# The start of a four-layer image kernel: first gram by transposes, rows copied inside its chain, weights made later, two banks for the first mixing products

## The chip, the cores and the metric

The kernel runs on one core of a Trainium2 chip. The core has five instruction streams: TensorE (PE, with weight loads listed as PEld), VectorE (DVE), ScalarE (ACT), GpSimd (POOL) and SyncE (SP). SP issues nearly all of the transfers; POOL and ACT issue some. The metric is the device time of one execution in microseconds, the median of several runs. The profile shows one further execution, instruction by instruction; its span reaches from the first to the last instruction.

## The reference, cut to what matters

The input is `x`, 16 images of 64 channels of 128 x 128 pixels, in fp32. Four layers follow one another, each adding its result to its input after a group norm over pairs of channels:

```python
x = x + _L0_conv_ref(_gn(x), L0_conv_conv_w)       # gram = x x^T / N; y = gram x; out = conv_w y
x = x + _L1_conv_ref(_gn(x))                       # |Sobel x| + |Sobel y|, per channel
x = x + _L2_conv_ref(_gn(x), L2_conv_W, L2_conv_b) # 3x3 convolution of a shifted x
x = x + _L3_conv_ref(_gn(x), L3_conv_w_bin, ...)   # 3x3, 1x1, batch norm over all images, clip to 0..255
```

Layer 0 is linear once the 64 x 64 gram matrix of an image is known: the kernel turns it into one 64 x 64 mixing matrix, and the statistics of both first norms follow from the same gram. Layer 3's batch norm needs every image's product before any output can be written.

## The kernel before

**Staging.** Every image passes three stages, each over eight row chunks (`NS = 8` chunks of `R = 8` rows of each half of the image, the upper and lower half on 64 partitions each): `Front` (layer 0's mixing product and layer 1's Sobel), `Layer2` and `Layer3`. The loop `for step in range(steps)` at L911 walks through steps of four quarters `q`; image `b` enters `Front` at step `15 + 8 b`, with three steps of preparation before it, `Layer2` at 25 and `Layer3` at 35 (`starts`, L861). Nearly all instructions of these stages go through the class `InOrder` (its helper is L73, the line that the profile shows for them), which keeps each engine's instructions in the order of the program text. So the order of work on each engine is written out by hand, and nothing overtakes.

**The gram.** `Gram` (L407) runs ahead of `Front`. It loads image `b` with pixel rows on the partitions (`xr`: eight transfers of 512 KB, each of 8 channels, 512 bytes a run), and ACT copies each into `xw`, in which the channels of a pixel column lie side by side. Once all eight are copied, 128 small products accumulate the gram with the channel sums in `pg`, half of them into partitions 0 to 63 and half into 64 to 127. `gram_chain` (L301) then computes the mixing matrix `abd` and the coefficients `co` of the norm: a chain of small steps between PE and DVE through the tile `bank`, with two square roots on ACT inside `rstd`. Each `yield` lets the loop issue other work; `tick` (L252) moves the chain on once in a quarter. For images 0 and 1 the chain takes fewer yields than for later ones. Images 1 to 6 are loaded at two chunks a step (`pace`, L871), image 0 at one.

**Front.** `mix` (L470) makes a mixing product `po` of four rows per half (512 columns; `small_product`, L177, issues the two 64-channel halves, and each fp32 product appears in the trace as two instructions). The pool of `po` has one buffer, a PSUM bank. `prepare` (L475) lets ACT normalize a `po` into the ring `xh`, with the rows next to it copied to the neighbouring chunks. `sobel` (L527) is eight DVE instructions and two of ACT for each chunk; the first, `u<-xh`, needs the halo row of the next chunk's first `po`. At its first step, `Front` also loads two edge rows (`xe`) and stores one row of zeros, from `w0`, to a scratch tensor; this store waits for POOL's memset of `w0` (L216), and what follows it on SP waits behind it.

**Setup before the loop.** The constants `kc` (identity and averaging matrices, 611.5 KB) and five small vectors are loaded by SP (L119 to L133), the weights by ACT's queue. The weights of layer 3 are nine products of 64 x 64 through `bank` (L226) with six DVE copies into `w3` (L229); a sum of taps, two copies to `wm` and eight copies to the `packed` tiles complete the other weights (L214 to L238). POOL clears `xh`, `w2`, `w3`, `w0` and four difference tiles.

**The end.** After the last image's statistics, the kernel reads its two intermediate tensors from HBM, normalizes, adds and writes `out`.

Of the kernel before, what the change touches and what calls it, by code (L numbers as in the profile page):

```python
# [10 lines left out]
F32 = mybir.dt.float32  # L11
# [5 lines left out]
P = 128  # L17
# [3 lines left out]
R = 8  # L21
NS = HH // R
EARLY = 3
CP = 4
# [84 lines left out]
def tile_kernel(ctx: ExitStack, tc: tile.TileContext, x, cw_h, w2_t, b2, wbin_t, w1_t, b1, gamma, beta, consts, out):  # L109
# [6 lines left out]
    small = ctx.enter_context(tc.tile_pool(name="small", bufs=4))  # L116

    kc = cpool.tile([P, K_END], F32, name="kc")
    nc.sync.dma_start(kc, consts)  # L119

    def k(name):
        return kc[:, AT[name][0]:AT[name][1]]

    def load_const(src, shape, name):
        t = cpool.tile(shape, F32, name=name)
        nc.sync.dma_start(t, src)
        return t

    cwh = load_const(cw_h, [P, C], "cwh")
    b2_sb = load_const(b2, [P, 1], "b2_sb")  # L130
    b1_sb = load_const(b1, [P, 1], "b1_sb")
    gamma_sb = load_const(gamma, [P, 1], "gamma_sb")
    beta_sb = load_const(beta, [P, 1], "beta_sb")  # L133
    bn_sum = cpool.tile([P, B * NS], F32, name="bn_sum")
    bn_sq = cpool.tile([P, B * NS], F32, name="bn_sq")

# [35 lines left out]
    def cols(o):  # L172
        return slice(o * C, (o + 1) * C)
# [19 lines left out]


    xw = wpool.tile([P, W // 2, C + 1, 2], F32, name="xw")
    nc.gpsimd.memset(xw[:, :, C, :], 1.0)

    xh = wpool.tile([P, 3, R + 2, W + 2], F32, name="xh")
    nc.gpsimd.memset(xh, 0.0)
    junk = wpool.tile([P, R * W], mybir.dt.bfloat16, name="junk")  # L200
    wbd = wpool.tile([P, P], F32, name="wbd")
    nc.gpsimd.memset(wbd, 0.0)

    w2 = wpool.tile([P, 3, 3, P], F32, name="w2")
    w3 = wpool.tile([P, 3, 3, P], F32, name="w3")
    nc.gpsimd.memset(w2, 0.0)
    nc.gpsimd.memset(w3, 0.0)
    for slot, i, o, ky in TO_SLOTS:
        nc.scalar.dma_start(w2[i * C:(i + 1) * C, slot, :, o * C:(o + 1) * C], w2_t[:, ky])

    wm = wpool.tile([P, 3, P], F32, name="wm")
    for n in range(2):
        o = 1 - single(TO_SLOTS, n)[0]
        nc.vector.tensor_copy(wm[:, :, cols(o)], w2[:, n, :, cols(o)])  # L214
    w0 = wpool.tile([P, P], F32, name="w0")
    nc.gpsimd.memset(w0, 0.0)  # L216

    wb = work.tile([P, R + 1, W + 2], F32, tag="u", name="wb")
    wb = flat(wb)[0:C, 0:9 * C].rearrange("p (y x c) -> p y x c", y=3, x=3)
    w1 = work.tile([P, R, W + 2], F32, tag="e", name="w1", bufs=1)[0:C, 0, 0:C]  # L220
    nc.scalar.dma_start(wb, wbin_t)
    nc.scalar.dma_start(w1, w1_t)
    for ky in range(3):
        pw = sm(3 * C, rows=C).rearrange("p (k c) -> p k c", k=3)
        for kx in range(3):
            nc.tensor.matmul(pw[:, kx, :], wb[:, ky, kx, :], w1, start=True, stop=True)  # L226
        for slot, i, o, kk in TO_PAIRS:
            if kk == ky:
                nc.vector.tensor_copy(w3[i * C:(i + 1) * C, slot, :, o * C:(o + 1) * C], pw)  # L229

    packed = {}
    for name, w, table in (("pk2", w2, TO_SLOTS), ("pk3", w3, TO_PAIRS)):
        nc.vector.tensor_add(w[:, 2], w[:, 0], w[:, 1])
        packed[name] = wpool.tile([P, 2, C], F32, name=name)
        for n in range(2):
            o, i = single(table, n)
            for kx, half in ((1, i), (0, 1 - i)):
                nc.vector.tensor_copy(  # L238
                    packed[name][half * C:(half + 1) * C, n], w[i * C:(i + 1) * C, n, kx, o * C:(o + 1) * C]
                )  # L240

    diffs, twins = {}, {}
    for name in ("d2", "d3"):
        diffs[name] = wpool.tile([P, 2, CP, W + 2], F32, name=name)
        nc.gpsimd.memset(diffs[name], 0.0)
        twins[name] = wpool.tile([P, 2, CP, W + 2], F32, name=f"q{name}")
        nc.gpsimd.memset(twins[name], 0.0)


    chains = []  # L250
# [50 lines left out]
    def gram_chain(b, pg):  # L301
# [77 lines left out]
            yield  # L379
        pk = sm(1)  # L380
        small_product(pk, pp.rearrange("p s c -> p (s c)"), k("q"))
        yield
        bias = sv("bias")
        dve.tensor_copy(bias, av[:, 2:3])
        st1 = sv("st1", 2)
# [18 lines left out]
        dve.tensor_copy(co[:, 3:4], mean)  # L404
        lead[b] = abd, co

    class Gram:  # L407
        first, last = 0, NS + 1

# [3 lines left out]
        def at(self, i, q):  # L413
            b = self.b
            CG = C // 8
            if i < NS:
                if q == 0 and i != 1:
                    for m in range(i + (1 if i == 2 else 2) if i else 0, min(i + 3, NS)):
                        t = xin.tile([P, CG, W], F32, tag="xr", name=f"xr_{b}_{m}", bufs=3)
                        sp.dma_start(t, x[b].rearrange("c h w -> h c w")[:, m * CG:(m + 1) * CG, :])  # L420
                        self.xr[m] = t

                if q == 3 and i > 0:
                    for m in (0, 1) if i == 1 else (i,):
                        act.copy(
                            xw[:, :, m * CG:(m + 1) * CG, :].rearrange("p w c t -> p c w t"),
                            self.xr.pop(m).rearrange("p c (w t) -> p c w t", t=2),
                        )
                return
            n = 4 * (i - NS) + q  # L430
            if n == 0:
                self.pg = ps_g.tile([P, CP, W], F32, tag="g", name=f"pg_{b}")[:, 0, 0:C + 1]

            for _ in range(22 if n < 4 else 20 if n < 6 else 0):
                w = self.w
                s = w % 2
                pe.matmul(
                    self.pg[s * C:(s + 1) * C, :], xw[:, w // 2, 0:C, s], xw[:, w // 2, :, s],
                    start=(w < 2), stop=(w >= W - 2),
                )  # L440
                last[0] = s
                self.w += 1
            if n == 6:
                chains.append(gram_chain(b, self.pg))
# [5 lines left out]
    class Front:  # L450
# [17 lines left out]
            self.xs[i] = t  # L468

        def mix(self, i, g):  # L470
            po = ps_po.tile([P, CP, W], F32, tag="po", name=f"po_{self.b}_{i}_{g}")
            small_product(po, self.abd, self.xs[i][:, g * CP:(g + 1) * CP, :])
            self.po[i, g] = po

# [389 lines left out]
    def run(stage, b, i, q):  # L864
        if 0 <= b < B and stage.first <= i <= stage.last:
            if (stage, b) not in live:
                live[stage, b] = stage(b)
            live[stage, b].at(i, q)


    pace = {}  # L871
    at = 0
    for b in range(B):
        half = 1 <= b <= 2 * EARLY
        pace[b] = at, 2 if half else 1

        at += (NS // 2 if half else NS) + {0: 4, 2 * EARLY: 2}.get(b, 0)
    last_one = NS * (B - 1) + starts[0][1]
    steps = last_one + NS + 1

# [27 lines left out]
            loaded.append((yt, rt))  # L908
            fetched[0] += 1

    for step in range(steps):  # L911
        for q in range(4):
            for b in range(B):

                i = step - starts[2][1] - NS * b
                if 0 <= i < NS and q in (0, 2):
                    live[Front, b].sobel(i, f"first of {q}")
                if q == 3:
                    run(Layer2, b, step - starts[1][1] - NS * b, "first of 3")
            for stage, at in starts:  # L920
                for b in range(B):
                    run(stage, b, step - at - NS * b, q)
            if q == 3:
                for b in range(B):
                    run(Layer2, b, step - starts[1][1] - NS * b, "last of 3")
            for b in range(B):
                at, n = pace[b]
                for m in range(n):
                    v = 4 * n * (step - at) + n * q + m
                    run(Gram, b, v // 4, v % 4)  # L930
# [100 lines left out]
```

## Time and profile before

| what | value |
|---|---|
| median of 3 runs | 2827.53 us (2825.04 to 2830.61) |
| the profiled execution | 2829.05 us |
| its span | 2827.3 us |
| PE, DVE, ACT, POOL busy | 2241.5, 2200.4, 2120.5, 884.3 us |
| first gram's products on PE | 27.39 to 37.73 us |
| first Sobel instruction of image 0 on DVE | starts at 59.68 us |
| last stretch, without PE | 2381 to 2827.3 us, 414 GB/s |

A row of the page's groups or of a timeline names the line, the engine, the operation, the tiles as out<-in, the shapes and a count; after it stand the busy time, and in square brackets the idle time of the engine before it with what ended this. `SPq` marks the issue of a transfer, not its duration. PEclk is the clock that was granted to TensorE, as a share of full speed.

### The profile page before, as it was taken

The page shows a single profiled execution, that of the slowest core. Times are in us where ns is not written, and L with a number is a line of the kernel's source. Part 1 is how long each engine was busy: PE and PEld are TensorE (multiplying, and loading weights), DVE is VectorE, ACT ScalarE, POOL GpSimd, SP SyncE. Part 2 cuts the span into 40 slices and gives each one's busy share as a digit, 9 for nine tenths or more (in the row PEclk, how much of TensorE's full clock was granted, in tenths as well). Part 3 has the DMA queues.
Part 4 walks back from the last instruction along what each step waited for, and adds up shares of the span by engine and source line. Part 5 has one row for each costly group of instructions (what it writes and reads, how often), then busy time and mean ns, then how long its engine had stood idle before and what let it go on. Part 6 is the DMA issues. An engine that isn't in the chain of part 4 may idle for free. (4 is left out here: it accounts for less than half of the span.)

```text
span 2827.3 us, 46297 instructions
## 1 busy us (share of the span) xinstructions
PE 2241.5 (79%) x14772; PEld 1157.1 (41%) x14772; DVE 2200.4 (78%) x3758; ACT 2120.5 (75%) x3171; POOL 884.3 (31%) x1326
## 2 busy tenths in 40 slices
PE   4568899999999999999999999999999995000000
PEld 2333444545453535363646363566666641000000
DVE  3999999898989898989898989999996434333332
ACT  4666779888888888888888888998997666333332
POOL 1035433343434343434343434454444300000000
PEclk8678999999999999999999999999999997555555
DMA  6788978888888888888888877888877668999999
GB/s 166 192 219 227 235 199 237 213 232 205 229 209 224 213 221 215 220 216 223 215 221 216 220 183 191 207 207 213 208 209 186 156 201 285 419 420 420 420 420 391
DMA packets 688880, 685.95 MB, mean 243 GB/s; under 512 B 61744, under 2 KB 590144, under 8 KB 688640
## 3 DMA queue, kind: packets, MB, share of 16 engines
q1 hardware_dynamic: 662656, 614.42, 73.7%
q0 software_dynamic: 24576, 68.12, 9.8%
q8 instruction: 119, 1.95, 0.3%
q14 instruction: 121, 0.99, 0.1%
q10 hardware_dynamic: 1408, 0.46, 0.1%
HBM read 346.23 MB, written 268.44 MB: 217 GB/s over the span
## 5 line engine op out<-in xcount | busy, mean ns | idle before, releaser
L73 PE MATMUL two<-d,w 128*64 128x508 f32 (+2 forms) x2560 | 894.2, 588 | 5.8 <-DVE d L73 5.8
L73 PE MATMUL two<-d,wi 128*64 128x508 f32 (+3 forms) x1536 | 620.1, 577 | 0.0
L73 POOL DMA_DIRECT2D qd<-d x512 | 269.8, 529 | 870.8 <-issue 318.4
L73 PE MATMUL two<-qd,pk 128*64 128x512 f32 (+1 forms) x1024 | 520.3, 589 | 3.2 <-DMA qd<-d 2.1
L73 POOL TENSOR_SCALAR edges<-v,co 64x8 f32<-64x8 f32 x512 | 348.8, 681 | 357.9 <-ACT v L73 248.7
L73 PEld LDWEIGHTS two<-d,w 128*64 128x64 f32 x2560 | 305.3, 136 | 285.5 <-issue 194.7
L73 PE MATMUL po<-x,abd 128*64 128x512 f32 x1024 | 369.8, 629 | 61.6 <-ACT xh L73 60.6
L73 DVE TENSOR_TENSOR d<-v 128x512 f32<-128x512 f32 (+1 forms) x512 | 345.9, 678 | 75.3 <-issue 36.0
L73 PE MATMUL one<-v,w 128*64 128x508 f32 (+2 forms) x1600 | 394.7, 578 | 0.0
L73 PE MATMUL one<-v,wi 128*64 128x508 f32 (+3 forms) x1536 | 391.4, 593 | 0.0
L73 ACT COPY qd<-d 64x512 f32<-64x512 f32 x512 | 315.3, 616 | 30.1 <-DVE d L73 23.7
L73 DVE SCALAR_TENSOR_TENSOR e<-e 128x1032 f32<-128x1032 f32 (+1 forms) x256 | 312.7, 1222 | 0.0
L73 ACT ACTIVATE xh<-po,co 128x128 f32<-128x128 f32 (+1 forms) x480 | 275.1, 621 | 40.8 <-PE po L73 38.8
L73 DVE SCALAR_TENSOR_TENSOR y<-two,c 128x1024 f32<-128x1024 f32 x128 | 155.8, 1217 | 132.0 <-ACT v L73 44.2
L73 PEld LDWEIGHTS two<-d,wi 128*64 128x64 f32 x1536 | 195.7, 136 | 145.2 <-issue 97.7
L73 POOL TENSOR_SCALAR v<-v,kc 128x9 f32<-128x9 f32 x256 | 249.7, 988 | 11.9
L73 PEld LDWEIGHTS one<-v,w 128*64 128x64 f32 x1600 | 171.9, 137 | 159.3 <-issue 97.5
L73 ACT ACTIVATE v<-x,co 128x512 f32<-128x512 f32 (+2 forms) x368 | 234.9, 704 | 0.0
L73 PEld LDWEIGHTS one<-v,wi 128*64 128x64 f32 x1536 | 163.0, 139 | 154.2 <-issue 110.1
L73 ACT ACTIVATE u<-u 128x1024 f32<-128x1024 f32 x128 | 135.5, 1058 | 96.7 <-DVE u L73 96.3
L73 DVE SCALAR_TENSOR_TENSOR u<-xh 128x1170 f32<-128x1170 f32 x128 | 175.5, 1371 | 12.2 <-ACT xh L73 9.8
L73 PEld LDWEIGHTS po<-x,abd 128*64 128x64 f32 x1024 | 110.8, 140 | 174.3 <-ACT xh L73 93.1
(154 smaller groups left out, 3476.0 us busy)
## 6 DMA issues: line engine op xcount, KB each, us to landing
xr<-in_x SPq DMA_DIRECT2D x128, 512.0 KB, 6.6
x<-in_x SPq DMA_DIRECT2D x256, 256.0 KB, 4.2
x_d<-u SPq DMA_DIRECT2D x512, 128.0 KB, 3.6
y_d<-y SPq DMA_DIRECT2D x512, 128.0 KB, 4.3
x_d<-x SPq DMA_DIRECT2D x496, 128.0 KB, 2.5
qd<-d POOLq DMA_DIRECT2D x256, 130.0 KB, 3.1
qd<-d POOLq DMA_DIRECT2D x256, 129.8 KB, 3.6
v<-x_d SPq DMA_DIRECT2D x448, 72.1 KB, 3.0
```

Source lines behind the costliest of these rows:

```text
L73: return self.tc.keep_in_program_order(call(*args, **kwargs))
```

## The change

`first_gram` replaces `Gram` for image 0. The image comes in the layout of `Front` (16 transfers of 256 KB with 4 KB runs). For each of eight chunks, PE turns eight 128 x 128 squares with the identity into two PSUM banks (`turned`), DVE and ACT each copy one half into `xw`, and the 16 products of a chunk follow those of the next chunk's transposes. A Sqrt on a dummy value comes first on ACT. Then the first step of `Front` 0 is issued, then the eight `xr` loads of image 1 (into buffers of the tag `x3`, whose earlier readers are the transposes), and the chain of image 0 runs in one go, with image 1's copies placed between its links on ACT, and two after it. The loop starts at step 13.

The identity columns of `kc` are loaded by SP; the rest of `kc` and all other constants and weights by POOL's queue, and the order of the memsets is changed: `w0` now follows the weights' loads. Layer 3's weight products and the other weights become two functions called in step 14 after quarter 1. `po_0_0` and `po_0_1` share one two-bank tile of the tag `two`. One yield of `gram_chain` is dropped for images 0 and 1.

```diff
-    nc.sync.dma_start(kc, consts)
...
+    sp.dma_start(kc[:, 0:P], consts[:, 0:P])
+    pool.dma_start(kc[:, P:K_END], consts[:, P:K_END])
+    for t, src in ((wb, wbin_t), (w1, w1_t), (cwh, cw_h)):
+        pool.dma_start(t, src)
...
+    pool.memset(wbd, 0.0)
...
+    pool.memset(w3, 0.0)
...
+    pool.memset(xh, 0.0)
+    pool.memset(w2, 0.0)
+    for t, src in ((b2_sb, b2), (b1_sb, b1), (gamma_sb, gamma), (beta_sb, beta)):
+        pool.dma_start(t, src)
+    for slot, i, o, ky in TO_SLOTS:
+        pool.dma_start(w2[i * C:(i + 1) * C, slot, :, o * C:(o + 1) * C], w2_t[:, ky])
+    w0 = wpool.tile([P, P], F32, name="w0")
+    pool.memset(w0, 0.0)
...
+    def weights_of_layer_3():
+        for ky in range(3):
+            pw = sm(3 * C, rows=C).rearrange("p (k c) -> p k c", k=3)
+            for kx in range(3):
+                pe.matmul(pw[:, kx, :], wb[:, ky, kx, :], w1, start=True, stop=True)
+            for slot, i, o, kk in TO_PAIRS:
+                if kk == ky:
+                    dve.tensor_copy(w3[i * C:(i + 1) * C, slot, :, o * C:(o + 1) * C], pw)
...
+    def other_weights():
+        for n in range(2):
+            o = 1 - single(TO_SLOTS, n)[0]
+            dve.tensor_copy(wm[:, :, cols(o)], w2[:, n, :, cols(o)])
...
         pk = sm(1)
         small_product(pk, pp.rearrange("p s c -> p (s c)"), k("q"))
-        yield
+        if b > 1:
+            yield
...
+    def first_gram():
+
+        pg = ps_g.tile([P, CP, W], F32, tag="g", name="pg_0")[:, 0, 0:C + 1]
+        src = []
+
+        t = sv("sd")
+        dve.memset(t, 1.0)
+        act.activation(t, t, AF.Sqrt)
+        for m in range(NS):
+            t = ring.tile([P, 2, CP, W], F32, tag="x3", name=f"x_first_{m}", bufs=NS + 2)
+            t = t.rearrange("p a j w -> p (a j w)")
+            for h in range(2):
+                sp.dma_start(t[h * C:(h + 1) * C], halves(x[0].rearrange("c h w -> (c h w)"), h, m * R, R))
+            src.append(t)
+        for m in range(NS + 1):
+            if m < NS:
+                two = ps_two.tile([P, 2, CP, W], F32, tag="two", name=f"turned_{m}").rearrange("p a j w -> p (a j) w")
+                for j in range(R):
+                    pe.transpose(two[:, j], src[m][:, j * P:(j + 1) * P], k("I"))
+                for h, copy in ((0, dve.tensor_copy), (1, act.copy)):
+                    copy(xw[:, m * R:(m + 1) * R, 0:C, h], two[:, :, h * C:(h + 1) * C])
+            if m > 0:
+                for w in range(2 * R * (m - 1), 2 * R * m):
+                    gram_product(pg, w)
+        run(Front, 0, Front.first, 0)
+
+        rows = []
+        for m in range(NS):
+            t = ring.tile([P, C // 8, W], F32, tag="x3", name=f"xr_1_{m}", bufs=NS + 2)
+            sp.dma_start(t, x[1].rearrange("c h w -> h c w")[:, m * C // 8:(m + 1) * C // 8, :])
+            rows.append(t)
+        for link, _ in enumerate(gram_chain(0, pg)):
+            if link in (2, 3, 4, 5, 6, 7):
+                rows_to_columns(1, link - 2, rows[link - 2])
+        for m in range(6, NS):
+            rows_to_columns(1, m, rows[m])
...
         def mix(self, i, g):
-            po = ps_po.tile([P, CP, W], F32, tag="po", name=f"po_{self.b}_{i}_{g}")
+            if self.b == i == 0:
+
+                if g == 0:
+                    self.two = ps_two.tile([P, 2, CP, W], F32, tag="two", name="po_0_0")
+                po = self.two[:, g]
+            else:
+                po = ps_po.tile([P, CP, W], F32, tag="po", name=f"po_{self.b}_{i}_{g}")
...
+    first_gram()
...
-    for step in range(steps):
+    for step in range(starts[2][1] - 2, steps):
...
+            if step == starts[2][1] - 1 and q == 1:
+                weights_of_layer_3()
+                other_weights()
```

More of the change, by code (lines that the diff above doesn't have):

```diff
@@ L118, in tile_kernel, with const @@
     kc = cpool.tile([P, K_END], F32, name="kc")
-    nc.sync.dma_start(kc, consts)
     def k(name):
         return kc[:, AT[name][0]:AT[name][1]]
[L124 to L133, printed above, removed]
+    def const(shape, name):
+        return cpool.tile(shape, F32, name=name)
+    cwh = const([P, C], "cwh")
+    b2_sb, b1_sb, gamma_sb, beta_sb = (const([P, 1], n) for n in ("b2_sb", "b1_sb", "gamma_sb", "beta_sb"))
     bn_sum = cpool.tile([P, B * NS], F32, name="bn_sum")
@@ L195, in tile_kernel @@
     xw = wpool.tile([P, W // 2, C + 1, 2], F32, name="xw")
[L196 to L216, printed above, removed]
+    pool.memset(xw[:, :, C, :], 1.0)
     wb = work.tile([P, R + 1, W + 2], F32, tag="u", name="wb")
@@ L220, in tile_kernel @@
     w1 = work.tile([P, R, W + 2], F32, tag="e", name="w1", bufs=1)[0:C, 0, 0:C]
[L221 to L240, printed above, removed]
+    sp.dma_start(kc[:, 0:P], consts[:, 0:P])
+    pool.dma_start(kc[:, P:K_END], consts[:, P:K_END])
+    for t, src in ((wb, wbin_t), (w1, w1_t), (cwh, cw_h)):
+        pool.dma_start(t, src)
+    junk = wpool.tile([P, R * W], mybir.dt.bfloat16, name="junk")
+    wbd = wpool.tile([P, P], F32, name="wbd")
+    pool.memset(wbd, 0.0)
+    w2 = wpool.tile([P, 3, 3, P], F32, name="w2")
+    w3 = wpool.tile([P, 3, 3, P], F32, name="w3")
+    pool.memset(w3, 0.0)
+    xh = wpool.tile([P, 3, R + 2, W + 2], F32, name="xh")
+    pool.memset(xh, 0.0)
[6 more added lines that the diff above has]
+    pool.memset(w0, 0.0)
     diffs, twins = {}, {}
@@ L244, in tile_kernel @@
         diffs[name] = wpool.tile([P, 2, CP, W + 2], F32, name=name)
-        nc.gpsimd.memset(diffs[name], 0.0)
+        pool.memset(diffs[name], 0.0)
         twins[name] = wpool.tile([P, 2, CP, W + 2], F32, name=f"q{name}")
-        nc.gpsimd.memset(twins[name], 0.0)
+        pool.memset(twins[name], 0.0)
+    def weights_of_layer_3():
[6 more added lines that the diff above has]
+                    dve.tensor_copy(w3[i * C:(i + 1) * C, slot, :, o * C:(o + 1) * C], pw)
+    wm = wpool.tile([P, 3, P], F32, name="wm")
+    packed = {}
+    def other_weights():
+        for n in range(2):
+            o = 1 - single(TO_SLOTS, n)[0]
+            dve.tensor_copy(wm[:, :, cols(o)], w2[:, n, :, cols(o)])
+        for name, w, table in (("pk2", w2, TO_SLOTS), ("pk3", w3, TO_PAIRS)):
+            dve.tensor_add(w[:, 2], w[:, 0], w[:, 1])
+            packed[name] = wpool.tile([P, 2, C], F32, name=name)
+            for n in range(2):
+                o, i = single(table, n)
+                for kx, half in ((1, i), (0, 1 - i)):
+                    dve.tensor_copy(
+                        packed[name][half * C:(half + 1) * C, n], w[i * C:(i + 1) * C, n, kx, o * C:(o + 1) * C]
+                    )
     chains = []
@@ L405, in gram_chain, with gram_product, rows_to_columns @@
         lead[b] = abd, co
+    def gram_product(pg, w):
+        s = w % 2
+        pe.matmul(
+            pg[s * C:(s + 1) * C, :], xw[:, w // 2, 0:C, s], xw[:, w // 2, :, s],
+            start=(w < 2), stop=(w >= W - 2),
+        )
+        last[0] = s
+    def rows_to_columns(b, m, t):
+        act.copy(
+            xw[:, :, m * C // 8:(m + 1) * C // 8, :].rearrange("p w c t -> p c w t"),
+            t.rearrange("p c (w t) -> p c w t", t=2),
+        )
+    def first_gram():
[31 more added lines that the diff above has]
+            rows_to_columns(1, m, rows[m])
     class Gram:
@@ L424, in at @@
                     for m in (0, 1) if i == 1 else (i,):
[L425 to L428, printed above, removed]
+                        rows_to_columns(b, m, self.xr.pop(m))
                 return
@@ L434, in at @@
             for _ in range(22 if n < 4 else 20 if n < 6 else 0):
[L435 to L441, printed above, removed]
+                gram_product(self.pg, self.w)
                 self.w += 1
@@ L868, in run @@
             live[stage, b].at(i, q)
+    first_gram()
     pace = {}
[L872 to L877, printed above, removed]
+    at = 12
+    for b in range(1, B):
+        pace[b] = at, 2 if b <= 2 * EARLY else 1
+        at += NS // pace[b][1] + (2 if b == 2 * EARLY else 0)
     last_one = NS * (B - 1) + starts[0][1]
@@ L925, in tile_kernel @@
                     run(Layer2, b, step - starts[1][1] - NS * b, "last of 3")
-            for b in range(B):
+            for b in range(1, B):
                 at, n = pace[b]
@@ L929, in tile_kernel @@
                     v = 4 * n * (step - at) + n * q + m
-                    run(Gram, b, v // 4, v % 4)
+                    if b > 1 or v >= 4 * NS:
+                        run(Gram, b, v // 4, v % 4)
+            if step == starts[2][1] - 1 and q == 1:
+                weights_of_layer_3()
+                other_weights()
             tick()
```

## The prediction

> **What bounds the kernel now.** I read the page first: the span, the busy digits by slice and the chain that ended last; then a table of busy times by stretch, then the timelines of the first 82 us, since every edit but one acts before step 16.
>
> ```profile
> span 2827.3 us, 46297 instructions
> PE   4568899999999999999999999999999995000000
> DVE  3999999898989898989898989999996434333332
> DMA 14%; ACT 1%; DVE 0%; PE 0%; issue 0%; SPq 0%; ACTq 0%
> ```
>
> The chain of the page starts at 2361 us and says only that the last 446 us are DMA. It does not reach the change. The stretches do (columns: length, busy time with count on PE, PEld, DVE, ACT, POOL; clock; DMA share; GB/s):
>
> ```profile
> 0.00:60.00 60.00, 23.27 (x330) 16.42 (x332) 13.92 (x64) 21.74 (x25) 9.79 (x15) 0.86 0.71 174
> 60.00:130.00 70.00, 42.23 (x610) 25.54 (x606) 64.99 (x102) 42.57 (x59) 0.40 (x2) 0.66 0.66 168
> 130.00:800.00 670.00, 617.33 (x4435) 285.56 (x4437) 621.65 (x1148) 554.67 (x843) 273.69 (x389) 0.95 0.86 222
> 800.00:2381.00 1581.00, 1558.67 (x9407) 829.54 (x9402) 1344.70 (x2319) 1345.10 (x2118) 600.39 (x921) 1.00 0.79 209
> 2381.00:2827.30 446.30, 0.00 (x0) 0.00 (x0) 155.15 (x129) 156.47 (x128) 0.00 (x0) 0.50 1.01 414
> ```
>
> DVE, then PE, is full from 60 to 2381 us; in the first 60 us no engine is. The instruction order of every engine after step 16 is the same in both kernels except around the second image's chain, so whatever the first Sobel step of image 0 gains or loses should arrive at the end whole. I call its start S (59.68 us now) and the start of the copy of the first gram E (37.79 us now). The timeline, in order of time:
>
> ```profile
> 6.46 14.68 SPq L73 DMA_DIRECT2D xr<-in_x  x8
> 22.55 0.48 SPq L73 DMA_DIRECT2D x_d<-w  x1
> 27.39 10.34 PE L73 MATMUL pg<-xw 128*64 128x65 f32 x256 [15.33 <-ACT xw L73]
> 37.79 0.23 DVE L73 COPY gs<-pg 128x65 f32<-128x65 f32 x1 [21.21 <-PE pg L73]
> 47.85 1.92 PE L73 MATMUL po<-x,abd 128*64 128x512 f32 x4
> 48.34 3.20 ACT L73 COPY xw<-xr 128x1024 f32<-128x1024 f32 x3
> 53.22 1.97 PE L73 MATMUL po<-x,abd 128*64 128x512 f32 x4 [3.44 <-ACT xh L73]
> 56.42 1.98 PE L73 MATMUL po<-x,abd 128*64 128x512 f32 x4 [1.23 <-ACT xh L73]
> 58.44 1.13 ACT L73 ACTIVATE xh<-po,co 128x512 f32<-128x512 f32 x2 [1.04 <-PE po L73]
> 59.68 1.38 DVE L73 SCALAR_TENSOR_TENSOR u<-xh 128x1170 f32<-128x1170 f32 x1 [9.85 <-ACT xh L73]
> ```
>
> So: 26 us of loads and copies with PE idle, 10.34 us of products in one piece, a chain of 10.44 us to its second Sqrt (48.23), three copies of image 1's rows in front of the first activation (3.20 us), and PE and ACT taking turns on one bank. From E to S it is 21.89 us.
>
> **What the Trainium skill says.** "TensorE: Matmul & The Clock Gate", Part 4, gives a transpose 390 ns alone and about 275 ns in a kernel, for bf16; the page's Terms say that the transpose mode is four times faster for FP32, and its section on LDWEIGHTS prices a load at columns / 1.2 GHz, so 107 ns for 128 columns. This trace holds no transpose. Part 1's two clock states are there: the same 65-column product pieces ran at 46 ns each (4.09 us for 88) and then 32 ns (5.40 us for 168). "DMA: Bandwidth & Descriptors", Specifications, wants 512 B runs for line rate; here 512 B rows of xr moved at 213 to 295 GB/s and the end's 4 KB rows at 414.
>
> **The change part by part.** All against the profiled execution: 2829.05 us around a span of 2827.3; the median of the runs, 2827.53, is 1.5 lower, and I take the difference over to it.
>
> *First gram.* Removed: eight xr loads, eight ACT copies, the wait until all have come. Added on SP: 64 KB of identity and 16 half loads of 256 KB in 4 KB rows; at 0.55 us an issue (1.10 for two) the first chunk is issued by 2.2 and its second half, begun at 1.67, lands 4.2 us later (median of the page's x row): 5.9. All 4.19 MB, with 0.75 MB of POOL's loads beside them, take 12 us at 414 GB/s, so the last chunk is there by about 15 to 16. On PE: 64 transposes T and 128 products, in the order T T G T G … G G. The products cost 10.34 us (1.29 a chunk). T is the unknown. Below: 0.107 us, the column load alone. Above: an ordinary fp32 product of 128 columns, two instructions of 0.25 us in the slow clock (four bank<-kc,vv took 1.01 us at 92.67), 0.50. I take 0.15, what one such instruction takes in the fast clock (0.60 us for four at 41.25), as the FP32 mode speaks for a single pass. The copies out of PSUM (DVE and ACT each 512 columns, near the 0.77 us of xh<-po) lie beside the next chunk's PE work; only the last shows. E = 5.9 + 64×0.15 + 10.34 + 0.77 = 26.6. PE is then the limit, not the loads.
>
> *Rows of image 1.* The eight copies (1.15 us each) leave the stretch after the chain: six stand on ACT between the two Sqrts (6.9 us in a gap of 8.2), two after. But their loads now queue on SP behind xe, behind the store of zeros from w0, and behind x_0, and the w0 memset has moved behind 14 DMA issues on POOL: 0.95 + 5.7 us of memsets + 14×0.52 (the qd<-d row) = 14 us; 20 if the six w2 issues with three runs a row cost three times that. Then 1.6 us of issues and 5.2 MB (x_0, xr, x_1) at 285 GB/s plus a latency: x_1 lands about 21 us after w0, at 35 to 41; row 5 at 30 to 36, before the second Sqrt at 37. The first activation moves to about 40, and five ACT pieces (0.45, 0.45, 0.76, 1.13, 1.13) are done by 44.
>
> *Two banks.* po_0_0, po_0_1 and po_1_0 no longer wait for ACT (3.44 and 1.23 us): by the rows above they end at E+11.98, +13.95 and +15.93.
>
> *Weights later.* This is not free. On PE nine products follow po_1_0 and stand before po_1_1; on DVE 16 instructions stand right before the first Sobel one. Three rounds of 0.90 (PE) and 0.72 (two DVE copies), with handovers, 5.1 us; then two wm copies 0.58, two adds 1.10, eight pk copies 1.58: 3.3. So S = E+15.93+8.4 = E+24.3. Before, they ran from 6.9 to 16.6 us under the loads at no cost; now they take back the two banks' gain and more (21.89 before).
>
> *Second chain.* One yield less: DVE waits once for pk's product, about 0.5 us; its tail moves before some Sobel work, same total.
>
> Sum: S = 26.6+24.3 = 50.9, 8.8 earlier, less 0.5: 8.3. Span 2819.0, profiled execution 2820.7, median 2819.2.
>
> **The rivals.** *All goes fast:* T 0.107 and products at 32 ns a piece (8.2 us): E = 21.8, S = 46.1, near the loads' own bound (x_1 at 35 + 1.98 + 8.4 = 45.4): 13 us less, 2814. For it: the loads do allow it. Against: the first pieces run at the slow clock.
>
> *Transposes about 0.21 to 0.28, or SP late:* load and stream one after the other at 1.2 GHz, 0.213, give E = 30.7 and a gain of 4; 0.275 gives none. A w0 at 24 us gives S = 24+31.3 = 55, again a gain of 4. Median 2823 to 2828.
>
> *Slower, by the price of a transpose:* place, PE between 6 us and E. From T = 0.28 nothing is left (E = 34.9), and from 0.37 it is slower by more than 0.2%. At 0.39 E is 42 and the median 2834; at 0.50, 2841. For it: no fp32 transpose is in the trace, the one number for bf16 alone is that large, and each loads new weights. Against: durations of overlapping instructions are longer than their spacing (LDWEIGHTS of two<-d,w: 136 ns mean, while the gram's pairs came every 40).
>
> **How the numbers follow.** Likeliest 0.42 (2815.5 to 2822), all fast 0.18, the middle case 0.25, slower 0.15. The runs before span 2825.04 to 2830.61, and 0.2% is 5.65 us, about what a measurement of this kernel can tell. Faster: the first two, and a little of the third less the likeliest's upper edge: 0.61. Same: 0.25. Slower: 0.14. The range goes from the fast case less 2 us of spread, 2812, to just short of the 0.39 case, 2832.
>
> **What would show it.** E near 26 and S near 51 in the new timeline; PE without long waits on DMA between 6 and E; 128-column transposes spaced 0.15 us, eight in 1.2; DVE's w3, wm and pk copies ending right at S, the first Sobel instruction released by DVE rather than by ACT; and the 2321 us from S to the last stretch (2381 − 60) unchanged. Wrong if transposes come in two instructions of 0.2 us, if PE's po waits for x_1 (then SP is the limit and the x_d<-w issue stands late), or if ACT's second Sqrt waits for a row.

## The result, and the profile after

| kernel | median (lowest to highest) | runs | ratio to before, 95% interval |
|---|---|---|---|
| after | 2825.27 us (2821.45 to 2827.68) | 20 | 0.9989 (0.9982 to 0.9996) |
| before, same chip | 2828.72 us (2821.70 to 2832.86) | 20 | |
| after, a second time | 2825.73 us (2824.57 to 2828.25) | 13 | 0.9993 (0.9985 to 1.0001) |
| before, same chip | 2828.02 us (2824.59 to 2833.95) | 25 | |

The change gives 3.4 us, and 2.3 us when measured again: within the 0.2% that the prediction called no difference to be told, though the first interval lies below 1. The forecast was 8.3 us. The profiled execution of after took 2827.62 us around a span of 2825.8; before's took 2829.05 around 2827.3.

The stretches of the start after the change, with the columns as in the table of before (length; busy time and count on PE, PEld, DVE, ACT, POOL; clock; DMA share; GB/s):

```profile
0.00:60.00 60.00, 34.66 (x398) 23.97 (x400) 17.68 (x71) 20.60 (x29) 17.98 (x29) 0.78 0.81 188
60.00:130.00 70.00, 39.25 (x592) 24.11 (x590) 64.21 (x101) 38.46 (x54) 0.40 (x2) 0.63 0.60 154
```

PE does 11.4 us more in the first 60 us (34.66 against 23.27). DVE has eight copies out of PSUM more, 0.69 us each (17.68 against 13.92 us in all), and is full no sooner. The timeline of after, in order of time, shows where the start stands:

```profile
1.18 15.28 SPq L73 DMA_DIRECT2D x_first<-in_x  x16
9.65 3.79 PE L73 MATMUL turned<-kc,x_first 128*128 128x128 f32 x16 [9.65 <-DMA x_first<-in_x]
14.52 1.09 PE L73 MATMUL turned<-kc,x_first 128*128 128x128 f32 x8
21.97 1.06 PE L73 MATMUL turned<-kc,x_first 128*128 128x128 f32 x8 [0.61 <-DMA x_first<-in_x]
42.40 0.20 ACT L73 ACTIVATE sd<-var 128x1 f32<-128x1 f32 x1 [0.56 <-DVE var L73]
45.58 1.15 ACT L73 COPY xw<-xr 128x1024 f32<-128x1024 f32 x1 [1.94 <-DMA xr<-in_x]
46.76 0.46 ACT L73 ACTIVATE xh<-pe,co 64x128 f32<-64x128 f32 x1
48.41 3.68 PE L73 MATMUL po<-x,abd 128*64 128x512 f32 x8 [4.46 <-ACT xh L73]
52.02 0.90 PE L73 MATMUL bank<-w,wb 64*64 64x64 f32 x6
59.43 0.79 DVE L73 COPY pk<-w 64x64 f32<-64x64 f32 x4
60.25 1.38 DVE L73 SCALAR_TENSOR_TENSOR u<-xh 128x1170 f32<-128x1170 f32 x1
```

The copy of the first gram starts at E = 31.24 us (37.79 before): 6.55 us gained. The first Sobel instruction starts at S = 60.25 us (59.68 before): all of it is given back, and 0.57 us more. A second profile of after has E = 31.23 and S = 58.80, two of before 59.68 and 59.35. Of the 1.45 us between the two profiles of after, 0.95 lie between the end of `po_1_0` and S: the same weight products took 0.90, 0.90 and 0.90 us in one and 0.63, 0.56 and 0.56 us in the other, where the granted clock from 52 to 56 us was 0.50 and 0.89. So the start is worth nothing within a microsecond, and the 2 to 3 us of the median come from elsewhere; the last experiments are about that.

Four readings follow from these lines. The first transposes wait 9.65 us for their chunk. Eight transposes take 1.09 us from the third chunk on, and 1.9 us in each of the first two. The write of `po_0_1`, which was to have its own bank, waits 4.46 us for ACT to read `po_0_0`. And the weights fill DVE up to S itself: the first Sobel instruction has no idle time before it.

### The profile page after: what moved, and what is told of

The parts are those of the page before. It is cut to its first block, busy times and chain, and to the rows that moved or that the text cites. A ratio compares the mean times of both kernels' runs of the same rounds, so it can differ in the third digit from the quotient of the medians.

```text
span 2825.8 us, 46448 instructions
## 1 busy us (share of the span) xinstructions
PE 2251.2 (80%) x14836; PEld 1162.2 (41%) x14836; DVE 2205.7 (78%) x3767; ACT 2115.0 (75%) x3171; POOL 893.3 (32%) x1340
## 3 DMA queue, kind: packets, MB, share of 16 engines
q8 instruction: 120, 1.97, 0.3%
```

## Experiments

"After" and "before" are whole kernels; an edit is against the one named. Ratios are to before on the same chip.

**The weights, both ways.** First, after with layer 3's three rounds (three products and two copies each) between the gram's chunks, and the other weights at the end of `first_gram`, ahead of the loop:

```diff
+    def weights_of_layer_3(taps_y):
+        for ky in taps_y:
...
+            if m in (3, 4, 5):
+                weights_of_layer_3([m - 3])
...
+        other_weights()
...
-            if step == starts[2][1] - 1 and q == 1:
-                weights_of_layer_3()
-                other_weights()
```

> The changed kernel with only the weights moved: layer 3's three rounds between the chunks of the first gram, the other weights on DVE between the end of the chain and the first Sobel step. Theory (the start counts whole, and DVE's weights hold the first Sobel step): S is then set by ACT's halo row of po_1_0, which ended at 53.3 us in the changed kernel's trace, so S near 53.5 to 54.5 instead of 60.25, and the median 6 to 7 us below the changed kernel's 2825.3, at 2818 to 2819.5. Rival (the difference between the kernels is made in the tail, where y waits for its store, and the start has slack): S moves the same, but the median stays at 2824 to 2827.

Measured: 2818.71 us (2814.82 to 2819.57), ratio 0.9966 (0.9952 to 0.9979). Its timeline:

```profile
19.07 0.56 PE L73 MATMUL bank<-w,wb 64*64 64x64 f32 x6
52.25 1.38 DVE L73 SCALAR_TENSOR_TENSOR u<-xh 128x1170 f32<-128x1170 f32 x1 [5.21 <-ACT xh L73]
```

A round between chunks costs PE 0.56 us. E is 31.41, as in after, though the three rounds took 1.7 us: PE waited only 0.40 us for later chunks in place of 1.52, and the first chunk happened to come 0.95 us earlier in this profile (8.70 against 9.65). S comes 8.0 us earlier (6.6 against the second profile of after) and waits for ACT, not for DVE's weights. It is 1.25 us before the expected 53.5, mostly since the last row's copy waited 0.71 us, not 1.94, for its load. The theory held: the median is 8.2 us below before on its own chip, which is 4.7 to 5.9 us more than after's two gains (6 to 7 expected).

Then the other way: in the kernel before, the setup's nine products and 18 DVE instructions for the weights go into step 14, with nothing else of the change:

```diff
-    for ky in range(3):
...
+            if step == starts[2][1] - 1 and q == 1:
+                weights_of_layer_3()
+                other_weights()
```

> The kernel before with one part of the change alone: the weights made in step 14, as in the changed kernel. Theory (on DVE they stand ahead of the first Sobel step and nothing hides them there): S goes from 59.68 to about 58.4 + 8.3 = 66.7, and the median rises by about 7 us, to 2835.5 (ratio 1.0025). Rival (slack later on takes it up): S rises but the median stays within 2 us of before.

Measured: 2833.4 us (2828.76 to 2835.39), ratio 1.0022 (1.0013 to 1.0031), S = 67.56. From its timeline:

```profile
66.73 0.79 DVE L73 COPY pk<-w 64x64 f32<-64x64 f32 x4
67.56 1.38 DVE L73 SCALAR_TENSOR_TENSOR u<-xh 128x1170 f32<-128x1170 f32 x1
```

It is 6.5 us slower, from a shift of S by 7.88, and the Sobel instruction again follows DVE's weights without idle time. This part of the change is a loss on its own, and of the size that the prediction gave it (8.4 us).

**Two tiles in place of one tile of two banks.** After, with `po_0_0` and `po_0_1` in two tiles of the tag `two`:

```diff
-                if g == 0:
-                    self.two = ps_two.tile([P, 2, CP, W], F32, tag="two", name="po_0_0")
-                po = self.two[:, g]
+                po = ps_two.tile([P, 2, CP, W], F32, tag="two", name=f"po_0_0_{g}")[:, 0]
```

> The changed kernel with po_0_0 and po_0_1 in two tiles of two banks each instead of two halves of one tile; all else as it is. Theory (the wait of 4.46 us in front of po_0_1 comes from the shared tile: a write to one half waits for ACT's read of the other): PE makes po_0_0, po_0_1 and po_1_0 in one piece, only x_1's landing between them, the weights start near 48 instead of 52.0, S near 56 instead of 60.25, median 3.5 to 4.5 us below the changed kernel. Rival (PE waited for something else that ended then, such as x_1 or the row copies): the wait stays and S stays at 60.

Measured: 2821.85 us (2819.29 to 2824.71), ratio 0.9983 (0.9975 to 0.9991). Its timeline:

```profile
42.24 3.05 PE L73 MATMUL po<-x,abd 128*64 128x512 f32 x8
46.82 1.08 PE L73 MATMUL po<-x,abd 128*64 128x512 f32 x4 [1.52 <-DMA x<-in_x]
47.45 2.79 ACT L73 ACTIVATE xh<-po,co 128x512 f32<-128x512 f32 x5
55.04 1.38 DVE L73 SCALAR_TENSOR_TENSOR u<-xh 128x1170 f32<-128x1170 f32 x1
```

Now both products of chunk 0 run in one piece, ahead of ACT, and what holds the third is a load. `po_1_0` ends at 47.90 instead of 52.09 us: these 4.2 us (3.7 against the second profile of after) are what the shared tile withheld, because the write of one half was ordered behind the read of the other. S is 5.21 us earlier; the last 1.0 us comes from the weight rounds, which took 0.56 us each on PE here and 0.90 in after (granted clock from 48 to 52 us: 0.93). Against before on its own chip the median gains 5.0 us, which is 1.6 to 2.7 more than after's two gains and less than the 3.5 to 4.5 expected.

**The first image by transfers over 128 partitions.** After, with one load a chunk over all partitions (rows of the upper and lower half interleaved, so the copies out of PSUM take every second column):

```diff
-            for h in range(2):
-                sp.dma_start(t[h * C:(h + 1) * C], halves(x[0].rearrange("c h w -> (c h w)"), h, m * R, R))
+            sp.dma_start(t, x[0].rearrange("c (h r) w -> (c h) (r w)", h=2)[:, m * R * W:(m + 1) * R * W])
...
-                    copy(xw[:, m * R:(m + 1) * R, 0:C, h], two[:, :, h * C:(h + 1) * C])
+                    copy(xw[:, m * R:(m + 1) * R, 0:C, h], two[:, :, h:P:2])
```

> The changed kernel with the first image loaded by eight transfers over all 128 partitions (512 KB, 4 KB runs, partition 2c+h) instead of 16 over 64 partitions; the copies out of PSUM take every second column; the bytes are the same. Theory (a transfer into 64 partitions gets about half of the bandwidth): the loads go at 350 GB/s or more instead of 205 to 250, the first chunk is there by about 6.5 us instead of 9.6, PE no longer waits for DMA between the chunks, E falls from 31.2 to 24 to 25.5; S then follows the second image's rows and falls by about 4 to 5 us, since the store from w0 still waits for POOL until 18 us. Rival (the rate is that of the HBM reads or of POOL's small loads beside them): the rate and E stay within 1.5 us.

Measured: 2819.07 us (2817.79 to 2821.72), ratio 0.9973 (0.9963 to 0.9983); E = 27.74, S = 54.70. From its timeline:

```profile
4.93 1.94 PE L73 MATMUL turned<-kc,x_first 128*128 128x128 f32 x8 [4.93 <-DMA x_first<-in_x]
8.54 1.97 PE L73 MATMUL turned<-kc,x_first 128*128 128x128 f32 x8 [1.68 <-DMA x_first<-in_x]
12.38 1.77 PE L73 MATMUL turned<-kc,x_first 128*128 128x128 f32 x8
```

The first chunk came even before the expected 6.5 us, but E fell by 3.5 us only, not to 24 to 25.5: PE still waited 1.68 us for the second chunk, and the first three chunks ran at 1.8 to 2.0 us for eight transposes. This edit halves the number of transfers too, so a further kernel takes the two apart, with two column halves a chunk:

```diff
-            sp.dma_start(t, x[0].rearrange("c (h r) w -> (c h) (r w)", h=2)[:, m * R * W:(m + 1) * R * W])
+            for h in range(2):
+                a = slice(h * R * W // 2, (h + 1) * R * W // 2)
+                sp.dma_start(t[:, a], x[0].rearrange("c (h r) w -> (c h) (r w)", h=2)[:, m * R * W:(m + 1) * R * W][:, a])
```

> The kernel load_128 with each of its eight loads cut into two transfers of 256 KB again, but by columns: both transfers of a chunk go over all 128 partitions (2 KB a partition). It tells the number of transfers from the partitions that one reaches, which load_128 changed together. Theory (64 partitions a transfer set the rate): first transposes near 5 us, 330 to 415 GB/s from 4 to 14 us, E within 1 us of load_128's 27.74, the median near 2819 to 2821. Rival (16 issues of 256 KB are slow by themselves): first transposes near 9 us, 16 issues in some 15 us, E near 31, the median near that of after.

Measured: 2818.64 us (2816.04 to 2821.5), ratio 0.9968 (0.9957 to 0.998); E = 26.67, S = 52.71. The stretch from 4 to 14 us (columns as above; its rate takes in POOL's loads), and in it the queue q1, which carries SP's loads (packets, MB, share of the DMA engines' time). After:

```profile
4.00:14.00 10.00, 4.20 (x36) 3.69 (x38) 1.21 (x2) 0.62 (x1) 9.63 (x11) 1.00 1.03 260
q1 hardware_dynamic: 564, 1.86, 78.0%
```

The kernel with 16 transfers over 128 partitions, and its first transposes:

```profile
4.00:14.00 10.00, 7.79 (x88) 6.45 (x88) 2.08 (x3) 1.47 (x3) 9.63 (x11) 1.00 1.04 355
q1 hardware_dynamic: 1619, 2.96, 87.1%
4.23 1.09 PE L73 MATMUL turned<-kc,x_first 128*128 128x128 f32 x4 [4.23 <-DMA x_first<-in_x]
7.04 1.12 PE L73 MATMUL turned<-kc,x_first 128*128 128x128 f32 x4 [1.73 <-DMA x_first<-in_x]
```

The DMA share is about 1.0 in both, at 260 GB/s in the first kernel and 355 in the second. SP's loads alone moved 1.86 MB in these 10 us, 186 GB/s, and 2.96 MB, 296 GB/s. (In steps of 2 us the totals are 235 to 288 and 291 to 388 GB/s; from 6 to 8 us they are nearly equal, 288 and 291, and there the expected 330 was missed.) With as many transfers of the same size, the median from issue to landing is 6.5 us in place of 10.2. The first transposes start at 4.23 us, not 9.65, but there half a chunk is enough for them; the second half's follow at 7.04. So it is not the number or size of the transfers; what is left is the partitions that one transfer reaches. (The addresses read changed with them, 2 KB pieces 32 KB apart in place of 4 KB pieces 64 KB apart; that was not tested apart.) The Trainium skill has this in "SBUF — State Buffer", "Door 1: The DMA port swizzle": partitions 0 to 63 reach 8 of the 16 ports, with 196 GB/s measured and 218 as the asymptote. Its section "Can I just issue two DMAs to hit both halves?" gives a gain of only 6% for two transfers, one on each half. The trace agrees: 186 GB/s for SP's loads into alternating halves.

**The zeros first.** After, with `w0` and its memset moved to the front of POOL's list:

```diff
+    w0 = wpool.tile([P, P], F32, name="w0")
+    pool.memset(w0, 0.0)
...
-    w0 = wpool.tile([P, P], F32, name="w0")
-    pool.memset(w0, 0.0)
```

> The kernel after with w0 and its memset moved to the front of POOL's list, so that the store of zeros no longer waits for 14 DMA issues and five memsets: w0 done by 2 us instead of 18, the store issued once xe's issues are through, and x_0 and the eight xr loads behind it about 3 to 4 us earlier. Theory (the late rows stand in front of the first activation): the copy of row 7 no longer waits 1.94 us for its load, the first activation comes 1.5 to 2.5 us earlier, S near 57.5 to 58.5, the median 1 to 2.5 us below that of after (some 2823). Rival (SP's 16 issues of x_first, up to 16.5 us, and the queue's rate set when the rows land, not the store): the rows land less than 1 us earlier and S stays within 0.7 us of 60.

Measured: 2825.69 us (2824.0 to 2828.05), ratio 0.9995 (0.9986 to 1.0003), S = 59.64. The rival held. From its timeline:

```profile
0.88 0.20 POOL L73 MEMSET w<- 128x128 f32 x1
1.18 14.49 SPq L73 DMA_DIRECT2D x_first<-in_x  x16
19.37 0.30 SPq L73 DMA_DIRECT2D x_d<-w  x1
23.14 14.91 SPq L73 DMA_DIRECT2D xr<-in_x  x8
44.97 1.15 ACT L73 COPY xw<-xr 128x1024 f32<-128x1024 f32 x1 [1.86 <-DMA xr<-in_x]
```

The zeros are ready at 1 us in place of 18, and the store still stands at 19.37 (20.84 in after), behind SP's own issues of `x_first` (to 15.67) and `xe` (to 18.20). In after, SP spent 11.4 of its first 26 us waiting for earlier loads of `x_first` to land, and none waiting for the zeros. The last row copy waits 1.86 us as before. In load_128, where the first image is through sooner, the `xr` issues begin at 17.59 and six row copies run in one piece of 6.30 us: it was the first image's loads that made the rows late. With those loads fast the zeros do count: in load_128 SP waits 6.2 us for POOL before this store.

**All four edits at once**, `load_128` with the two tiles, the early weights and the zeros first:

```diff
+            sp.dma_start(t, x[0].rearrange("c (h r) w -> (c h) (r w)", h=2)[:, m * R * W:(m + 1) * R * W])
...
+            if m in (3, 4, 5):
+                weights_of_layer_3([m - 3])
...
+                po = ps_two.tile([P, 2, CP, W], F32, tag="two", name=f"po_0_0_{g}")[:, 0]
```

> The kernel after with four edits of its start together: the first image by 8 loads over 128 partitions, po_0_0 and po_0_1 in two tiles, the rounds of layer 3's weights between the gram's chunks and the other weights ahead of the loop, the memset of w0 first. Theory (the start's shifts arrive at the end one to one, and the three losses are separate): E near 27.5 as with the loads alone, S at 41 to 44 us, that is 16 to 18.5 us before that of the kernel before; with the tail's 3 us a median of 2807 to 2811. Rival (they share a cover, most likely the rows of image 1 on SP and ACT, so that one gain eats another): S at 47 or later, the median above 2813.

Measured: 2812.56 us (2810.47 to 2813.51), ratio 0.9944 (0.9932 to 0.9957): 15.5 us below before and 13 below after, the best of all kernels here. S is 46.29, later than the 41 to 44 expected, and S and median both lie nearer to the rival than to the theory. From its timeline:

```profile
29.64 0.23 DVE L73 COPY gs<-pg 128x65 f32<-128x65 f32 x1 [1.96 <-PE pg L73]
40.23 0.20 ACT L73 ACTIVATE sd<-var 128x1 f32<-128x1 f32 x1 [1.94 <-DVE var L73]
40.34 2.19 ACT L73 COPY xw<-xr 128x1024 f32<-128x1024 f32 x2
42.56 0.45 ACT L73 ACTIVATE xh<-pe,co 64x128 f32<-64x128 f32 x1
43.39 2.79 ACT L73 ACTIVATE xh<-po,co 128x512 f32<-128x512 f32 x5
46.29 1.38 DVE L73 SCALAR_TENSOR_TENSOR u<-xh 128x1170 f32<-128x1170 f32 x1 [1.51 <-ACT xh L73]
```

Two terms were missed. E is 29.64, 1.9 later than in load_128: with the loads faster PE has no spare time between the chunks, so the three rounds of 0.56 us are paid there (the first transposes were 0.34 us later too). And from 40.23 on ACT works without a pause: two row copies and seven activations, up to S. ACT is the next bound. In weights_early S waits for ACT as well, but there ACT itself waited 2.07 and 0.58 us for `po`; in the other kernels with one edit of after S follows DVE's weights.

**Where the 2 to 3 us of the median come from.** S was not earlier, so something later must be. The trace of before has two long waits in its tail, where `y` waits for the store of an earlier `y`, queued among the loads for the end; after has shorter ones. From the timelines, before:

```profile
2338.32 1.22 DVE L73 SCALAR_TENSOR_TENSOR y<-two,c 128x1024 f32<-128x1024 f32 x1 [8.46 <-DMA y_d<-y]
2350.82 1.23 DVE L73 SCALAR_TENSOR_TENSOR y<-two,c 128x1024 f32<-128x1024 f32 x1 [10.06 <-DMA y_d<-y]
```

After:

```profile
2336.42 1.23 DVE L73 SCALAR_TENSOR_TENSOR y<-two,c 128x1024 f32<-128x1024 f32 x1 [5.67 <-DMA y_d<-y]
2348.02 1.23 DVE L73 SCALAR_TENSOR_TENSOR y<-two,c 128x1024 f32<-128x1024 f32 x1 [9.16 <-DMA y_d<-y]
```

The order of SP's and POOL's instructions there is the same in both; the places of the tiles in SBUF are not. The kernel before_layout has before's instructions with after's places:

```diff
+    xh = wpool.tile([P, 3, R + 2, W + 2], F32, name="xh")
+    w0 = wpool.tile([P, P], F32, name="w0")
...
+    for m in range(16):
+        ring.tile([P, 2, CP, W], F32, tag="x3", name=f"pre_{m}", bufs=NS + 2)
```

> The kernel before with every instruction and its order unchanged; only the places of the tiles in SBUF differ: the weight tiles are allocated in the order of the kernel after, and the rotation of the buffers of x3, xe and x begins where it stands after first_gram there. Theory A (the 2 to 4 us that the tail between 2328 and 2352 us gives come from where the end's loads land in SBUF): S stays at 59.7, the two waits of y for its store in the tail fall from 8.46 and 10.06 us to about 5.7 and 9.2, the prefetch moves about 405 GB/s from 2325 to 2350 instead of 320 to 400, the median is 2.5 to 4 us below that of before. Theory B (the places in HBM, or the moment of the rival transfers, or chance): S 59.7, the tail as before, the median within 1.5 us of before.

Measured: 2828.28 us (2824.99 to 2833.16), ratio 1.0001 (0.9993 to 1.0009). Its tail is short (the two waits are 6.43 and 9.13 us), as theory A says, but its median is that of before. Its profile loses 3.4 us elsewhere, at 267 us, where ACT waits for a store:

```profile
278.10 1.35 ACT L73 ACTIVATE v<-v,co 128x1154 f32<-128x1154 f32 x1 [7.48 <-DMA x_d<-x]
```

A second profile of each of three kernels, with no edit, tells chance from kernel:

> The kernel before, unchanged, profiled a second time: a measure of what two profiles of one kernel differ by. If the long tail (steps of 10.9 and 12.5 us after 2327 us, both waits of y for its store) belongs to the program and its places in SBUF, it comes again within 0.5 us, with S at 59.7 and the end of the statistics at 2381. If it is chance: a tail with a step near 8.9 and 11.6 us, as before_layout showed. The median within 1 us of before either way.

> The kernel before_layout, unchanged, profiled a second time. In its first profile 3.4 us were lost at 267 us, where ACT waited 7.48 us for a store of x_d, and 2.7 us won in the tail. If the loss is chance and the win belongs to the layout: no loss at 267, the end of the statistics near 2378.5, and a median 1 to 3 us below before. If the win was chance too: tail steps near 10.9 and 12.5, and the same median. If both belong to the layout: both come again, and the same median.

> The kernel after, unchanged, profiled once more beside the others. If the tail's gain belongs to the program: S near 60.3, steps of 8.1 and 11.6 us in the tail, the statistics' end 2 to 3 us before that of before, and the median 2 to 4 us below before. If it was the chance of one profile: tail steps of 11 and 12.5 us in this one.

Measured: before_again 2826.17 us, ratio 0.9997 (0.9989 to 1.0005); layout_again 2828.51 us, 1.0005 (0.9996 to 1.0013); after_again as in the first table. In the profiles of one kernel the waits move about. In after_again the two waits in the tail are 6.69 and 10.10 us, where after has 5.67 and 9.16, though its statistics end 1.5 us earlier. From the timeline of before_again:

```profile
276.33 1.35 ACT L73 ACTIVATE v<-v,co 128x1154 f32<-128x1154 f32 x1 [5.86 <-DMA x_d<-x]
2338.92 1.23 DVE L73 SCALAR_TENSOR_TENSOR y<-two,c 128x1024 f32<-128x1024 f32 x1 [6.21 <-DMA y_d<-y]
2350.63 1.22 DVE L73 SCALAR_TENSOR_TENSOR y<-two,c 128x1024 f32<-128x1024 f32 x1 [9.27 <-DMA y_d<-y]
```

The same instruction of `v` in before:

```profile
273.28 1.35 ACT L73 ACTIVATE v<-v,co 128x1154 f32<-128x1154 f32 x1 [3.84 <-DMA v<-x_d]
```

So the same kernel lost its 3 us once in the tail and once at about 267 us. The end of the statistics (the start of the last `sh` on DVE) shows what remains:

| profile | S | end of statistics | from S to there |
|---|---|---|---|
| before, before_again | 59.68, 59.35 | 2381.01, 2380.94 | 2321.33, 2321.59 |
| before_layout, layout_again | 59.68, 59.87 | 2381.52, 2378.62 | 2321.84, 2318.75 |
| before_weights_late | 67.56 | 2386.92 | 2319.36 |
| after, after_again | 60.25, 58.80 | 2378.64, 2377.11 | 2318.39, 2318.31 |
| zero_first, weights_early | 59.64, 52.25 | 2377.66, 2369.76 | 2318.02, 2317.51 |
| two_tiles, load_128 | 55.04, 54.70 | 2372.51, 2370.08 | 2317.47, 2315.38 |
| load_128x16, all_start | 52.71, 46.29 | 2369.78, 2362.15 | 2317.07, 2315.86 |

All profiles of kernels with the change are shorter from S on than all of those without it, by 3.3 us in the mean, though layout_again and after differ by 0.4 only. The stretch after the statistics takes 0.8 us of this back: it lasts 447.1 to 447.5 us with the change and 446.1 to 446.9 without. That leaves 2.5 us, the order of after's gains of 3.4 and 2.3 us in the median. In the medians of the other kernels with the change, what is gained beyond the shift of S is 0.4 to 2.8 us.

Set against the profile of after, four of the five profiles without the change lose some 3 us in one such place, in the tail or at about 267 us; of the other seven with it none does (against before, those with it lose 1 to 2 us near 656 us and get 2 back by 1900). Why stays open. Places in SBUF alone are not enough (before_layout and layout_again have after's places, and the time of before), and the length of the tail changed between two profiles of the same kernel. Not tried was before with after's second chain or with its places in HBM.

## Why the prediction was right or wrong

The range 2812 to 2832 held the result. Of its three outcomes "same" came, which had been given 0.25, and not "faster" with 0.61. That 2825 lies in the middle case (2823 to 2828) was luck: that case asked for slow transposes or late zeros and a gain of 4 us at the start, and none of the three came. The likeliest sum, a gain of 8.3 us at the start, did not come either. S was to be 50.9 and was 60.25, 9.35 later; the 2 to 3 us that were gained arose after S, where nothing had been forecast. By its steps:

- **First gram: right in its transposes, wrong in its limit.** T was to be 0.15 us; each is one instruction, eight took 1.09 us, 0.136 each, and with the slow first sixteen the mean is 0.16. (The clock states read from before were off: the first 88 of its 256 product pieces took 4.80 us, 55 ns each, and the other 168 took 5.54, 33 ns each. E doesn't use them, only the all-fast case does.) "PE is then the limit, not the loads" is the step that failed. The first chunk was put at 5.9 us from an issue and the 4.2 us of a transfer alone, and the whole at 414 GB/s, the rate of the end's 128-partition transfers. It came at 9.65 (3.75 later), and PE waited 1.52 us more for three other chunks. E was 31.24 in place of 26.6. With loads over 128 partitions and as many transfers, E is 26.67. PE's own time was well foreseen: from its first transpose to E it took 20.5 us there without its 2.0 us of waits for loads, and 20.1 in after, for the 20.7 foreseen. That E agrees so closely is partly chance, since the first loads came 1.7 us earlier than foreseen and the waits took 2.0. The prediction read the length of the runs, 4 KB, but not the partitions; the faster kernel has runs of 2 KB.
- **Two banks: the step failed.** "po_0_0, po_0_1 and po_1_0 no longer wait for ACT" was read from the banks; but the wait belonged to the tile, and there was one tile. In after's order of instructions ACT's wait stands on the second product, and it was overlooked. `po_1_0` ended at E+20.85, not E+15.93. In two_tiles it ended at E+16.46, held by the load of `x_1`, which the prediction had named as a sign of being wrong.
- **Rows of image 1: the delay came, but not from the store.** The last row's copy waited 1.94 us and the first activation came at 46.76, not at about 40; 4.6 us of this came with E. The 14 to 20 us for `w0` was right (17.88), but zero_first shows that the store was not what held the rows. The slow loads of the first image were: their 16 issues took 15.28 us on SP, where the prediction priced one at 0.55.
- **Weights later: right.** 8.4 us foreseen, 8.2 measured from the end of `po_1_0` to S (7.2 in the second profile), and 8.0 and 7.9 when moved in either direction. The instructions on DVE are 18, not 16; the price had all 18.
- **Carried to the end whole: right in size.** Shifts of S by −13.4, −7.4, −7.0, −5.0, −4.6 and +7.9 us against before (all_start, weights_early, load_128x16, load_128, two_tiles, before_weights_late) became differences of the median of −15.5, −8.2, −9.2, −7.8, −5.0 and +6.5. That "the 2321 us from S to the last stretch" stay unchanged was wrong by some 3 us: they became 2315.4 to 2318.4, and that is where the profiles show the gain that was measured. What made it is open.
- **Second chain:** the 0.5 us could not be told apart from this spread.
- **The slower rival** fell with T. Its opposite, all fast, fell at E already: T was 0.16 in the mean, not 0.107, the products took 9.9 us, not 8.2, and the loads were not fast.

So the sum lost 4.6 us at E and 4.9 between E and `po_1_0`, and the late weights were then paid just as priced.

## What to carry to other kernels

A load that feeds a bound should go over all partitions in each transfer: transfers over 64 partitions each kept the DMA share near 1.0 at two thirds of the rate (186 against 296 GB/s). A DMA share near 1.0 does not say that the rate is the highest to be had. Two banks in one tile were ordered here as one buffer, so read the waits on the second write, not the number of banks. And a step that costs nothing under a wait is paid whole when the same change removes that wait or moves the step past it (the weights: nothing before, 8.2 us after).

## What the runs showed of the hardware that was not expected

- A transpose of 128x128 in fp32 is one instruction. In after 43 of the 64 appear in the trace with a duration of 272 to 273 ns, and eight in a row take 1.09 us, so the duration is twice the spacing; the first sixteen, before PE had been busy, took 3.79 us, 0.237 each (the 1.00 that the view gives for the clock in that time does not show this). The Trainium skill, "TensorE: Matmul & The Clock Gate", Part 4, says that the full clock is not engaged by transposes. Here they were mixed with products and sped up soon after these began (the third eight took 1.09 us in after, and still 1.97 in two_tiles), so the trace leaves that open.
- The profiles of one kernel differ by some 3 us in where a store keeps an engine waiting (267 us or 2338 us), while their ends agree within 0.1 us (2381.01 and 2380.94). One profile of each kernel would have laid the difference to the tail.
